# Attention's TensorE products issued in source order, in a block of a mixture of experts, attention and a second mixture

## The chip, the cores and the metric

The kernel runs on one core of a Trainium2 chip, in float32 throughout. A core has TensorE (matrix products, PE, with its weight loads PEld), VectorE (DVE), ScalarE (ACT), GpSimd (POOL) and SyncE (SP), which run side by side, each in the order of its own queue, and 16 DMA engines. Products land in PSUM, which has eight banks of 2 KB in each partition; all else lies in SBUF. The metric is the device time of one execution in microseconds (us), the median of some runs.

## The reference

Three residual steps on x of 2 x 1024 tokens with 512 features: half a mixture of experts, attention, half a mixture again. The change is in attention alone. Cut to what matters:

```python
x = x + 0.5 * ffn(layernorm(x))      # 2 experts, one per token, hidden 2048
x = x + attention(layernorm(x))
x = x + 0.5 * ffn(layernorm(x))

# attention: 16 heads, key width 64, value width 128, 64 slots a head
q, k, v = x @ Wq, x @ Wk, x @ Wv;  s = clip(x @ Ws, -32, 32);  g = x @ Wg
z = cumlogsumexp(s over time);  p = exp(s - z);  decay = exp(z[t-1] - z[t])
hk = hk * decay + k_t p_t^T          # per head, 64 x 64
ok_t = q_t hk / sqrt(64);  pv = softmax(ok over the slots)
hv = hv * decay + p_t v_t^T          # per head, 64 x 128
o_t = pv_t hv
o = rmsnorm(o) * g_norm_weight * g * sigmoid(g)
return o @ Wo
```

## The kernel before

Python code writes the whole program out without loops on the chip. A planner (the Tile framework) then sets the order of each engine's queue: it goes through the instructions with a time model of its own, gives an engine the earliest written one that is ready in the model, and adds all waits between engines. So the order on an engine may differ from that of the source. `tc.issue_after(ins)` binds instructions: what is written inside its block is put behind `ins` on the engine of `ins`, and adds no wait by itself. PSUM is guarded by bank. Pools give a tile name a number of buffers (`bufs`); a new tile waits until the last user of its buffer is done.

The first mixture runs to about 510 us, attention to 1965 us, the last mixture (its first steps inside attention's last units) to the end.

Attention works on 64 *units*: 2 sequences x 4 groups of 4 heads x 8 chunks of 128 tokens (c = 0 to 7). The state of a group is carried from chunk to chunk in `sk_st` and `sv_st`. Iteration i of the main loop (L1273) works on three units at once: *cur* is unit i, *mid* i-1, *old* i-2. An 8-chunk group repeats the same pattern.

Projections are made for two neighbouring units together, by a scheme with 7 products of half matrices in place of 8, as generators of which `next` takes a step:

- `values_gates` (L968): v and the gate sg of a pair, with banks U (tag ok), C and V (tag pj). The sums X of the tokens that it needs are made by DVE in `token_sums`. A product is 2 matmuls of 128x128 by 512 columns.
- `keys_slots` (L1015): k and E, the exponentials of the slots, of a pair. U and V are the two halves of one bank, `bank[:, 0]` and `bank[:, 1]`. ACT copies partial sums out (kp, kv, ku, L1024), DVE adds (L1033, L1042). A product is 2 matmuls by 256 columns.
- `queries` (L1057): once for 4 chunks, pq, 8 matmuls by 512 columns.

In an odd iteration the values of a later pair are made, in an even one the keys of *cur* and its neighbour, and the rest of the values.

The other products of a unit are small, each with a step of another engine behind it:

- `transpose_keys_slots` (tk), copied by ACT to kET; `running_sum` makes CT and its reciprocal rC on DVE.
- `scores` (Ap): products of 64 rows, two halves of the array one after the other in two banks (tag at, 2 buffers); DVE masks each to A (L1092).
- `slot_scores` (ok): for each of two pairs of heads the state product (sk, L1117, full array), then two products with A onto 64 columns each (L1122), all in one bank of tag at. DVE multiplies by rC to sT.
- `slot_softmax` (ts): transposes, maximum and subtraction on DVE, Exp on ACT to e.
- `transpose_u` (tu), DVE to uT; `update_key_state` (skp), DVE into sk_st.
- `slot_weights` (Bp): as Ap, masks to B. `outputs` (ov): state product (L1180), then products with B (L1186); ACT squares, DVE and ACT make the norm ms, POOL scales the gate sg (L1201), DVE multiplies to og (L1203).
- `update_value_state` (svp): products onto 64 columns each, DVE adds into sv_st. ts, skp and svp share one bank (tag st), to, tu and tk another (tag tr).
- `transpose_out` (to), ACT to oT; `project_out` (po): 4 matmuls by 512 columns, DVE adds to the rows x. In the last group it also calls `then.feed()`, which ranks finished tokens for the last mixture.

A matmul over all rows and columns of the array shows as 128*128 in the profile; Ap and Bp are 64*128, svp and the products of L1122 128*64. One fp32 product shows as two records, a transpose as one.

Source order of an iteration before: ok(mid); a projection step; ts(mid), to(old); steps; tu(mid), po(old); skp(mid), Bp(mid); steps; ov(mid), svp(mid); tk, running sum, queries, Ap of cur. The planner was free to mix them.

Of the kernel before, what the change touches and what calls it, by code (L numbers as in the profile page):

```python
# [49 lines left out]
def tile_macaron(  # L50
# [783 lines left out]
    class Attention:  # L834
        def __init__(self, ph):
            self.ph, self.rows, self.xT = ph, [None] * NBLK, [None] * NBLK
            self.vg, self.ks, self.q, self.o = {}, {}, {}, {}

        def norm(self, b):
# [99 lines left out]
    def attention(att, then, then_steps, weight_steps):  # L939
# [3 lines left out]


        def product(bank, left, right, start):
            for d in range(2):
                nc.tensor.matmul(  # L947
                    bank, lhsT=left[:, d], rhs=right[:, d],
                    start=start and d == 0, stop=d == 1, skip_group_check=True,
                )  # L950
# [17 lines left out]
        def values_gates(u):  # L968
# [21 lines left out]
            p1 = keep(U, "th", "p1")  # L990
            token_sums(u)
            C = ps2.tile([P, 512], F32, tag="pj", name=f"C{u.nm}")
            product(C, a12, B21, True)
# [21 lines left out]
        def keys_slots(u):  # L1015
            pair = u, units[u.n + 1]
            B11, B21, B22, T1, T2, T3, T4 = att.ks[u.b, u.g]
            a11, a12, a21, a22 = halves(u)
            bank = ps2.tile([P, 2, 256], F32, tag="pj", name=f"kU{u.nm}")
            U, V = bank[:, 0], bank[:, 1]  # L1020

            def keep(bank, tag):
                t = work.tile([P, 256], F32, tag=tag, name=f"{tag}{u.nm}", bufs=1)
                nc.scalar.copy(t, bank)  # L1024
                return t

            def key(v):
                v.k = work.tile([P, HG * DK], F32, tag="k", name=f"k{v.nm}")
                return v.k

            def slot(v, bank, other):
                v.E = work.tile([P, HG * M], F32, tag="E", name=f"E{v.nm}", bufs=3)
                nc.vector.tensor_tensor(v.E, bank, other, ALU.add)  # L1033
                nc.vector.tensor_scalar(v.E, v.E, -32.0, 32.0, ALU.max, ALU.min)
                nc.scalar.activation(v.E, v.E, AF.Exp)


            product(U, a11, B11, True)
            p1 = keep(U, "kp")
            C = ps2.tile([P, 256], F32, tag="pj", name=f"kC{u.nm}")  # L1040
            product(C, a12, B21, True)
            nc.vector.tensor_tensor(key(u), C, p1, ALU.add)  # L1042
            product(V, u.S[:, 0], T1, False)
            p5 = keep(V, "kv")
            product(U, u.S[:, 1], T2, False)
            u2 = keep(U, "ku")
            product(V, u.S[:, 3], B22, False)
            slot(u, V, u2)
            yield
            product(U, u.S[:, 2], T3, False)  # L1050
            slot(pair[1], U, p5)
            yield
            product(U, a22, T4, False)
            nc.scalar.copy(key(pair[1]), U)
            yield

        def queries(u, prev):  # L1057
# [4 lines left out]
            for pr in range(NPR):  # L1062
                pj = ps2.tile([P, 512], F32, tag="pj", name=f"pq{u.nm}_{pr}")
                for dc in range(DC):
                    c0 = dc * HG * DK + pr * P
                    nc.tensor.matmul(  # L1066
                        pj, lhsT=att.q[u.b, u.g][:, c0 : c0 + P], rhs=xT[u.blk][:, dc, :],
# [4 lines left out]
        def transpose_keys_slots(u):  # L1072
            tp = ps1.tile([P, 2 * NPR, P], F32, tag="tr", name=f"tk{u.nm}")
            for pr in range(NPR):
                nc.tensor.transpose(tp[:, pr, :], u.k[:, ts(pr, P)], ident)
                nc.tensor.transpose(tp[:, NPR + pr, :], u.E[:, ts(pr, P)], ident)
            u.kET = work.tile([P, 2 * NPR, P], F32, tag="kET", name=f"kET{u.nm}", bufs=3)
            nc.scalar.copy(u.kET, tp)

        def masked_products(u, name, lT, rT):  # L1080
# [3 lines left out]
            for j in range(2):  # L1084
                r = slice(j * 64, (j + 1) * 64)
                pp = ps2.tile([P, NPR, P], F32, tag="at", name=f"{name}p{u.nm}_{j}")
                for pr in range(NPR):
                    nc.tensor.matmul(
                        pp[:, pr, :], lhsT=lT[r, pr, :], rhs=rT[r, pr, :],
                        start=True, stop=True,  # L1090
                    )
# [20 lines left out]
        def slot_scores(u):  # L1112

            op = ps2.tile([P, NPR, P], F32, tag="at", name=f"ok{u.nm}")
            for pr in range(NPR):
                if u.c:
                    nc.tensor.matmul(  # L1117
                        op[:, pr, :], lhsT=sk_st[:, pr, :],
                        rhs=u.qT[:, pr, ts(u.c % 4, P)], start=True, stop=False,
                    )  # L1120
                for j in range(2):
                    nc.tensor.matmul(  # L1122
                        op[j * M : (j + 1) * M, pr, :],
                        lhsT=u.E[:, ts(2 * pr + j, M)], rhs=u.A[:, j * NPR + pr, :],
                        start=(u.c == 0), stop=True,
                    )
# [3 lines left out]
        def slot_softmax(u):  # L1130
            tp = ps1.tile([P, HG, M], F32, tag="st", name=f"ts{u.nm}")
            for pr in range(NPR):
                nc.tensor.transpose(
                    tp[:, 2 * pr : 2 * pr + 2, :].rearrange("p h m -> p (h m)"), u.sT[:, pr, :], ident
# [10 lines left out]
        def update_key_state(u):  # L1145
# [3 lines left out]
            for pr in range(NPR):  # L1149
                nc.tensor.matmul(  # L1150
                    sp[:, pr, :], lhsT=u.k[:, ts(pr, P)], rhs=u.E[:, ts(pr, P)],
# [10 lines left out]
        def transpose_u(u):  # L1162
            tp = ps1.tile([P, NPR, P], F32, tag="tr", name=f"tu{u.nm}")
            for pr in range(NPR):
                nc.tensor.transpose(
                    tp[:, pr, :], u.u[:, 2 * pr : 2 * pr + 2, :].rearrange("p h m -> p (h m)"), ident
# [9 lines left out]
        def outputs(u):  # L1176
            op = ps1.tile([P, HG, DV], F32, tag="ov", name=f"ov{u.nm}")
            for pr in range(NPR):
                if u.c:
                    nc.tensor.matmul(  # L1180
                        op[:, 2 * pr : 2 * pr + 2, :].rearrange("p h v -> p (h v)"),
                        lhsT=u.uT[:, pr, :], rhs=sv_st[:, pr, :],
                        start=True, stop=False,
                    )
                for h in (2 * pr, 2 * pr + 1):
                    nc.tensor.matmul(  # L1186
                        op[:, h, :], lhsT=u.Bm[:, h % 2 * NPR + pr, :], rhs=u.v[:, ts(h, DV)],
                        start=(u.c == 0), stop=(u.c == 0 or h % 2 == 1),
                    )

# [12 lines left out]
            nc.vector.tensor_tensor(u.og, op, sg, ALU.mult)  # L1203

        def update_value_state(u):
            if u.c == NC - 1:
                return
            sp = ps1.tile([P, NPR, DV], F32, tag="st", name=f"svp{u.nm}")
            for h in range(HG):
                j = h % 2  # L1210
                nc.tensor.matmul(  # L1211
                    sp[j * M : (j + 1) * M, h // 2, :],
                    lhsT=u.E[:, ts(h, M)], rhs=u.v[:, ts(h, DV)], start=True, stop=True,
                )
            for j in range(2):
                r, v = slice(j * M, (j + 1) * M), ts(j, DV)
                st = sv_st[r, :, v]
                if u.c == 0:
                    nc.vector.tensor_copy(st, sp[r, :, :])
                else:  # L1220
                    nc.vector.tensor_tensor(st, sp[r, :, :], st, ALU.add)  # L1221

        def transpose_out(u):
            tp = ps1.tile([P, HG, P], F32, tag="tr", name=f"to{u.nm}")
            for h in range(HG):
                nc.tensor.transpose(tp[:, h, :], u.og[:, h, :], ident)  # L1226
            u.oT = work.tile([P, HG, P], F32, tag="oT", name=f"oT{u.nm}")
            nc.scalar.activation(u.oT, tp, AF.Copy, scale=gnh)  # L1228

        def project_out(u):  # L1230
# [3 lines left out]
            for h in range(HG):  # L1234
                nc.tensor.matmul(  # L1235
                    pj, lhsT=u.oT[:, h, :], rhs=att.o[u.b, u.g][:, ts(h, D)],
# [33 lines left out]

        for _ in range(3):
            project_ahead(-1)
        for i in range(n + 2):  # L1273
# [3 lines left out]

            def step():
                if i >= n - 1:
                    next(then_steps)  # L1280

            if mid:
                slot_scores(mid)
            if cur:
                if i % 2:
                    project_ahead(i)
                else:
                    keys = keys_slots(cur)
                    next(keys)
            step()  # L1290
            if mid:
                slot_softmax(mid)
            if old:
                transpose_out(old)
            if cur:
                project_ahead(i)
                if i % 2 == 0:
                    next(keys)
            step()
            if mid:  # L1300
                transpose_u(mid)
            if old:
                project_out(old)
            step()
            if mid:
                update_key_state(mid)
                slot_weights(mid)
            if cur:
                project_ahead(i)
                if i % 2 == 0:  # L1310
                    ahead = None
                    next(keys)
            step()
            if mid:
# [3 lines left out]
                if mid.b == 0 and mid.c < 6 and mid.g < NG - 1:  # L1318
                    with tc.issue_after(mid.gated.ins):
                        next(weight_steps)  # L1320
                        next(weight_steps)
            step()
            if cur:
                transpose_keys_slots(cur)
                running_sum(cur, mid)
                queries(cur, mid)
                scores(cur)
                if cur.g == NG - 1 and cur.b == 0:
# [96 lines left out]
```

## Time and profile before

| what | us |
|---|---|
| median of 3 runs | 2398.35 (2397.66 to 2399.46) |
| the profiled execution, as timed | 2399.73 |
| its span, from first to last instruction | 2398.0 |
| TensorE busy in the span | 2333.1 |
| one pattern of 8 units, from the same product at 761.56 to that at 940.90 | 179.3 |
| TensorE busy from 1200 to 1300 | 99.85 |
| DVE busy from 1200 to 1300 | 61.23 |
| ACT busy from 1200 to 1300 | 39.59 |
| POOL busy from 1200 to 1300 | 8.26 |

The profile is of one execution. In its timelines a row is: start, length, engine, line, operation, what is written <- what is read, shapes, and how many records were merged into the row; brackets hold the engine's idle time before it and what ended that. The length of a TensorE row goes to the modelled end of its last product, which overlaps the next row: distances between starts tell how long TensorE was held. In the waits a row is: who waited <- for whom: us in total, times, longest.

### The profile page before, as it was taken

What the parts mean: (1) busy time and instruction counts of PE and PEld (TensorE: products, weight loads), DVE (VectorE), ACT (ScalarE), POOL (GpSimd) and SP (SyncE); (2) the same over time, 40 slices, a digit from 0 to 9 for tenths busy, and PEclk for the clock granted to TensorE, in tenths of its full rate; (3) what the DMA queues carried; (4) which work ended last, traced back from release to release, by engine and by line L of the source; (5) the groups of instructions that cost most, each with busy time, mean ns of one, the idle gap of its engine ahead of it and who ended that gap; (6) DMA issues with size and microseconds to landing.
All of it is one profiled execution on the core that took longest, in us unless ns stands there. A gap on an engine that the chain in (4) does not pass through costs nothing.

```text
span 2398.0 us, 28205 instructions
## 1 busy us (share of the span) xinstructions
PE 2333.1 (97%) x10552; PEld 1566.3 (65%) x10552; DVE 1366.1 (57%) x3116; ACT 784.1 (33%) x1470; POOL 466.6 (19%) x401
## 2 busy tenths in 40 slices
PE   7998999999999999999999999999999999999998
PEld 5686787865555556556556556556556578888865
DVE  6543556656546556557666545555557567766411
ACT  2221222323333333344443333333333432222222
POOL 3513616101101101100101000000000244634000
PEclk9999999999999999999999999999999999999999
DMA  7516335221311311310401200200100203313442
GB/s 286 211 64 247 142 106 213 75 103 45 123 57 44 127 54 45 110 58 23 163 27 49 80 27 14 80 27 14 62 1 36 106 18 154 106 62 132 158 171 97
DMA packets 56937, 222.70 MB, mean 93 GB/s; under 512 B 5983, under 2 KB 13151, under 8 KB 38880
## 3 DMA queue, kind: packets, MB, share of 16 engines
q1 hardware_dynamic: 51232, 203.52, 23.9%
q0 software_dynamic: 5280, 16.85, 1.8%
q8 instruction: 83, 1.36, 0.2%
q10 hardware_dynamic: 288, 0.52, 0.1%
q14 instruction: 54, 0.44, 0.1%
HBM read 189.86 MB, written 31.54 MB: 92 GB/s over the span
## 4 chain that ended last, share of the span: by engine, by line
PE 81%; DVE 10%; issue 5%; DMA 2%; POOL 1%; ACT 1%; SPq 0%; POOLq 0%; DVEq 0%; ACTq 0%
PE U L947 9%; PE po L1235 9%; PE kU L947 6%; PE oa L673 6%; PE hU L606 6%; PE V L947 5%; PE pq L1066 5%; PE o L673 4%; PE hp L509 4%; PE hV L606 3%; PE op L728 3%; PE C L947 2%; PE ok L1122 2%; PE ov L1186 2%; PE ov L1180 2%
## 5 line engine op out<-in xcount | busy, mean ns | idle before, releaser
L1201 POOL TENSOR_TENSOR sg<-sg,ms 128x512 f32<-128x512 f32 x64 | 66.5, 1039 | 1202.8 <-DVE ms L1199 1177.4
L1235 PE MATMUL po<-wo,oT 128*128 128x512 f32 x512 | 232.5, 593 | 0.6 <-ACT oT L1228 0.6
L509 PE MATMUL hp<-xsT,wfc 128*128 128x256 f32 (+1 forms) x768 | 150.6, 352 | 10.6 <-DMA wfc<-in_w_fc_dram 7.2
L509 PEld LDWEIGHTS hp<-xsT,wfc 128*128 128x128 f32 x768 | 129.0, 194 | 33.6 <-issue 15.4
L1235 PEld LDWEIGHTS po<-wo,oT 128*128 128x128 f32 x512 | 92.2, 191 | 88.2 <-issue 86.4
L728 PE MATMUL op<-wp,a 128*128 128x512 f32 x320 | 143.2, 593 | 0.0
L947 PE MATMUL U<-vgT,X 128*128 128x512 f32 x256 | 125.5, 593 | 0.0
L496 DVE SCALAR_TENSOR_TENSOR t<-hp,r 128x256 f32<-128x256 f32 (+1 forms) x96 | 36.3, 379 | 155.4 <-ACT r L495 155.1
L1240 DVE TENSOR_TENSOR x<-po,x 128x512 f32<-128x512 f32 x64 | 44.3, 691 | 136.6 <-PE po L1235 136.6
L1066 PE MATMUL pq<-xnT,wq 128*128 128x512 f32 x256 | 112.9, 593 | 0.0
L1110 DVE RECIPROCAL rC<-CT 128x256 f32<-128x256 f32 x64 | 111.6, 1744 | 0.3
L947 PE MATMUL kU<-ksT,X 128*128 128x256 f32 x384 | 105.8, 393 | 0.6 <-ACT kp L1024 0.6
L986 ACT ACTIVATE th<-sg 128x512 f32<-128x512 f32 x64 | 40.2, 629 | 183.9 <-DVE sg L984 183.6
L606 PE MATMUL hU<-xsT,wfc 128*128 128x256 f32 x384 | 100.0, 383 | 0.3 <-ACT e L613 0.3
L728 PEld LDWEIGHTS op<-wp,a 128*128 128x128 f32 x320 | 59.8, 191 | 60.8 <-issue 57.3
L947 PEld LDWEIGHTS kU<-ksT,X 128*128 128x128 f32 x384 | 68.5, 190 | 31.7 <-DVE E L1033 10.6
L495 ACT ACTIVATE r<-hp 128x256 f32<-128x256 f32 (+1 forms) x96 | 33.3, 347 | 156.5 <-PE hp L509 156.1
L1197 ACT ACT_TABLE_LOAD x55 | 70.6, 1283 | 41.8 <-DVE ms L1196 41.8
L1221 DVE TENSOR_TENSOR sv<-svp,sv 64x256 f32<-64x256 f32 x96 | 40.4, 421 | 76.9 <-PE svp L1211 74.7
L1186 PEld LDWEIGHTS ov<-v,B 128*128 128x128 f32 x512 | 76.5, 191 | 10.2 <-issue 3.3
L1228 ACT ACTIVATE oT<-to,gnh 128x512 f32<-128x512 f32 x64 | 43.6, 681 | 120.6 <-PE to L1226 120.3
L1066 PEld LDWEIGHTS pq<-xnT,wq 128*128 128x128 f32 x256 | 47.4, 191 | 52.7 <-issue 52.5
(296 smaller groups left out, 5168.2 us busy)
## 6 DMA issues: line engine op xcount, KB each, us to landing
wfc<-in_w_fc_dram SPq DMA_DIRECT2D x48, 1024.0 KB, 4.9
wp<-in_w_proj_dram SPq DMA_DIRECT2D x48, 1024.0 KB, 6.6
vgT<-vgs SPq DMA_DIRECT2D x16, 1024.0 KB, 5.2
wv<-in_w_v_dram SPq DMA_DIRECT2D x8, 1024.0 KB, 6.2
ksT<-kss SPq DMA_DIRECT2D x8, 1024.0 KB, 4.7
wo<-in_w_o_dram SPq DMA_DIRECT2D x8, 1024.0 KB, 6.1
xs<-xs SPq DMA_DIRECT2D x6, 1032.0 KB, 6.2
wks<-in_w_ks_dram SPq DMA_DIRECT2D x24, 256.0 KB, 4.1
```

Of the source, the lines that this page charges most:

```text
L509: m.mark = nc.tensor.matmul(hp, lhsT=wfc[:, dc * HQ + hc * P : dc * HQ + (hc + 1) * P], rhs=xT[:, dc, :], start=(dc == 0), stop=(dc == DC ...
L606: m.mark = nc.tensor.matmul(bank, lhsT=left[:, d, :], rhs=right[:, d, :], start=start and d == 0, stop=d == 1, skip_group_check=True,)
L673: nc.tensor.matmul(bank[:, t, :], lhsT=left(q)[:, ts(t, P)], rhs=right(q), start=first and q == 0 and (t == 0 or last), stop=last and q == ...
L728: nc.tensor.matmul(ops[j], lhsT=a[hc][:, ts(j, P)], rhs=wp[:, ts(hc, D)], start=(ck == 0 and hc == 0), stop=(ck == NHQ - 1 and hc == HQ // ...
L947: nc.tensor.matmul(bank, lhsT=left[:, d], rhs=right[:, d], start=start and d == 0, stop=d == 1, skip_group_check=True,)
L1066: nc.tensor.matmul(pj, lhsT=att.q[u.b, u.g][:, c0 : c0 + P], rhs=xT[u.blk][:, dc, :], start=(dc == 0), stop=(dc == DC - 1),)
L1110: nc.vector.reciprocal(u.rC, u.CT)
L1122: nc.tensor.matmul(op[j * M : (j + 1) * M, pr, :], lhsT=u.E[:, ts(2 * pr + j, M)], rhs=u.A[:, j * NPR + pr, :], start=(u.c == 0), stop=True,)
L1186: nc.tensor.matmul(op[:, h, :], lhsT=u.Bm[:, h % 2 * NPR + pr, :], rhs=u.v[:, ts(h, DV)], start=(u.c == 0), stop=(u.c == 0 or h % 2 == 1),)
L1197: nc.scalar.activation(ms, ms, AF.Sqrt, bias=eps, scale=1.0 / DV)
L1201: u.gated = then.gated = nc.gpsimd.tensor_tensor(sg, sg, ms.to_broadcast([P, HG, DV]), ALU.mult)
L1235: nc.tensor.matmul(pj, lhsT=u.oT[:, h, :], rhs=att.o[u.b, u.g][:, ts(h, D)], start=(h == 0), stop=(h == HG - 1),)
```

## The change

All of attention's products and transposes go through a helper that puts each one behind the one traced just before it. The generators of the projections get three more places to stop. `slot_scores` and `outputs` do all state products before the local ones (with flags that fit), `value_state_products` is taken out of `update_value_state` and put behind `slot_weights`, `update_key_state` goes ahead of `slot_weights` by a projection step, `transpose_out` goes ahead of `slot_softmax`, and `project_out` goes behind `queries`. The steps of the last mixture that run beside the last units stay five to an iteration.

```diff
+        def on_pe(op, *args, **kw):
+            with tc.issue_after(att.pe.ins) if att.pe else nullcontext():
+                att.pe = op(*args, **kw)
...
         def product(bank, left, right, start):
             for d in range(2):
-                nc.tensor.matmul(
+                on_pe(
+                    nc.tensor.matmul,
                     bank, lhsT=left[:, d], rhs=right[:, d],
...
         def values_gates(u):
             token_sums(u)
+            yield
             C = ps2.tile([P, 512], F32, tag="pj", name=f"C{u.nm}")
...
         def keys_slots(u):
             nc.vector.tensor_tensor(key(u), C, p1, ALU.add)
+            yield
             product(V, u.S[:, 0], T1, False)
             p5 = keep(V, "kv")
             product(U, u.S[:, 1], T2, False)
             u2 = keep(U, "ku")
+            yield
             product(V, u.S[:, 3], B22, False)
...
         def slot_scores(u):
+            for pr in range(NPR if u.c else 0):
+                on_pe(
+                    nc.tensor.matmul, op[:, pr, :], lhsT=sk_st[:, pr, :],
+                    rhs=u.qT[:, pr, ts(u.c % 4, P)], start=(pr == 0), stop=False,
+                    skip_group_check=True,
+                )
             for pr in range(NPR):
-                if u.c:
-                    nc.tensor.matmul(
-                        op[:, pr, :], lhsT=sk_st[:, pr, :],
-                        rhs=u.qT[:, pr, ts(u.c % 4, P)], start=True, stop=False,
-                    )
                 for j in range(2):
-                    nc.tensor.matmul(
-                        op[j * M : (j + 1) * M, pr, :],
+                    on_pe(
+                        nc.tensor.matmul, op[j * M : (j + 1) * M, pr, :],
                         lhsT=u.E[:, ts(2 * pr + j, M)], rhs=u.A[:, j * NPR + pr, :],
...
+        def value_state_products(u):
+            if u.c == NC - 1:
+                return
+            u.svp = ps1.tile([P, NPR, DV], F32, tag="st", name=f"svp{u.nm}")
+            for h in range(HG):
+                j = h % 2
+                on_pe(
+                    nc.tensor.matmul, u.svp[j * M : (j + 1) * M, h // 2, :],
+                    lhsT=u.E[:, ts(h, M)], rhs=u.v[:, ts(h, DV)], start=True, stop=True,
+                )
...
-        for _ in range(3):
+        for _ in range(4):
             project_ahead(-1)
```

The main loop after, in full up to the loads, which stay as they were:

```python
            def project(even, odd):
                if i >= n - 1:
                    next(then_steps)
                for step in (odd if i % 2 else even) if cur else "":
                    if step == "v":
                        project_ahead(i)
                    else:
                        next(keys)

            if cur and i % 2 == 0:
                keys = keys_slots(cur)
            project("k", "v")
            if mid:
                slot_scores(mid)
            project("k", "v")
            if old:
                transpose_out(old)
            if mid:
                slot_softmax(mid)
            project("kvk", "v")
            if mid:
                transpose_u(mid)
                update_key_state(mid)
            project("k", "v")
            if mid:
                slot_weights(mid)
                value_state_products(mid)
            project("v", "")
            if cur and i % 2 == 0:
                ahead = None
            if mid:
                outputs(mid)
                update_value_state(mid)
                ...
            if cur:
                transpose_keys_slots(cur)
                running_sum(cur, mid)
                queries(cur, mid)
            if old:
                project_out(old)
            if cur:
                scores(cur)
```

## The prediction

> **What bounds the kernel now.** I read the busy table and the slices first, then the chain, the waits of TensorE, and last the timeline of the attention stage (about 510 to 1965 us).
>
> ```profile
> span 2398.0 us, 28205 instructions
> PE 2333.1 (97%) x10552; PEld 1566.3 (65%) x10552; DVE 1366.1 (57%) x3116; ACT 784.1 (33%) x1470; POOL 466.6 (19%) x401
> PEclk9999999999999999999999999999999999999999
> PE 81%; DVE 10%; issue 5%; DMA 2%; POOL 1%; ACT 1%; SPq 0%; POOLq 0%; DVEq 0%; ACTq 0%
> DVE og L1203 <- POOL sg L1201: 54.2, 53, 1.2
> PE ok L1117 <- DVE A L1092: 6.5, 18, 1.0
> PE kU L947 <- ACT kp L1024: 0.6, 1, 0.6
> ```
>
> TensorE sets the time: 97% busy at the full granted clock, and in attention it waits for hardly anything (the last two lines, of the waits: us in total, times, longest; the line on DVE is used further down). So an order of its work can win only in how long the same products take, and lose only by new waits. The first is in the timeline of TensorE (start, length, line, records merged; one fp32 matmul is two records):
>
> ```profile
> 943.08 1.02 PE L947 MATMUL U<-vgT,X 128*128 128x512 f32 x2
> 944.03 0.43 PE L1122 MATMUL ok<-A,E 128*64 128x128 f32 x2
> 944.40 0.49 PE L1117 MATMUL ok<-qT,sk 128*128 128x128 f32 x2
> 944.82 0.44 PE L1122 MATMUL ok<-A,E 128*64 128x128 f32 x4
> 945.18 1.13 PE L947 MATMUL kU<-ksT,X 128*128 128x256 f32 x4
> ...
> 953.48 0.61 PE L1150 MATMUL skp<-E,k 128*128 128x128 f32 x4
> 954.02 0.72 PE L1088 MATMUL Bp<-uT,kET 64*128 64x128 f32 x8
> 954.67 1.98 PE L947 MATMUL U<-vgT,xnT 128*128 128x512 f32 x4
> ```
>
> Read the starts. Undisturbed, a full-array (128*128) record takes 0.43 us at 512 columns, 0.215 at 256, 0.108 at 128 (four skp records: 0.54 with what follows). But 943.08 to 944.03 is 0.95 for two records of 0.43: 0.10 more, because what follows uses half the array (128*64). The half-array records then end 0.15 late, and the first full-array record afterwards is 0.11 long (945.18: four records in 0.97 instead of 0.86). Each *excursion* to a half-array form costs this toll beside its work. I took it over all 363 excursions of attention from the matmul starts, from the full record before to the second one after, less the undisturbed times (half-array records counted at 53 ns, since two halves can run together): ok in 2 records 0.459 us (90 times; only one half is in use), ok in 4 records 0.367 (67), ok in all 8 0.364 (8), Bp in 8 0.430 (63), Ap in 8 0.440 (44), Ap in 4 0.405 (32), svp in 8 0.318 (51), svp run into Ap 0.630 (4; 0.589 median), odd ones 2.0 us. Sum 148.9 us.
>
> **What the change takes away.** Every attention matmul is put behind the one traced before it, and slot_scores now does its four state records first. So ok becomes one excursion of 8 for each of 64 units, Ap one of 8, and Bp with svp right behind it one of 16 (56 units; 8 last chunks have no svp). Priced by the rows: ok 64 x 0.363 = 23.2; Ap 64 x 0.427 (median) = 27.3; Bp+svp 56 x 0.589 = 33.0; Bp alone 8 x 0.429 = 3.4. Sum 86.9, so **62 us** less. The Bp+svp price is bounded by the four run-on pairs (0.589) and by two full tolls (0.429 + 0.363 = 0.79).
> The Trainium skill, "TensorEngine Tiling (Array Packing)", section Key Properties, says that changing the tiling mode, not just the tile, drains TensorE; Bp (64*128) to svp (128*64) changes it. By that rule the pair would pay 0.79, the sum of gains would be 11 us smaller and the time 2390.
> The old waits of ok and kU go too: 6.5 + 0.6, and the 0.11 us restart that I count 45 times behind a state product of ok that had to wait, and 37 times behind kU and U: 4.9 + 4.0. About **16 us**. Gains together 78 (62 to 78; 51 with two tolls).
>
> **What it adds.** Matmuls and their columns stay the same, value_state_products only moves; no DMA is added, and loads, stores and weight sums keep their places in the SP and POOL queues. The flags and the wrapper cost no instruction. project_out moves behind tk and queries; in the last group the feed (DVE, a ranking matmul, POOL scatters) goes with it. The last scatter now starts at 1970.97 and pass 1's tokens are worked on at 2009, so some us there are covered; without cover they would be paid once. What counts is that TensorE can no longer step past an instruction that waits. Place by place:
>
> 1. *Keys, second step* (32 pairs). U and V share a bank, and the planner lets no engine write one half while another reads the other:
>
> ```profile
> 1033.02 0.35 ACT L1024 COPY kp<-kU 128x256 f32<-128x256 f32 x1
> 1033.43 1.13 PE L947 MATMUL kU<-ksT,X 128*128 128x256 f32 x4 [0.63 <-ACT kp L1024]
> ...
> 1034.39 1.02 PE L947 MATMUL U<-vgT,X 128*128 128x512 f32 x2
> 1034.59 0.37 ACT L1024 COPY kv<-kU 128x256 f32<-128x256 f32 x1 [1.22 <-PE kU L947]
> ...
> 1035.25 1.03 PE L947 MATMUL kU<-ksT,X 128*128 128x256 f32 x4
> ```
>
> At 1033.43 product V waits for the copy kp of U, though they share no data. Between V and the next U there is now always a product of values (1034.39), which hides the copy kv. After the change V and U stand back to back in one step with nothing between: 0.20 us to the copy's start, 0.37, 0.06 to TensorE, 0.11 restart: 0.74. 32 x 0.74 = **23.7** (nothing in the row hides it; zero only if the planner tracked halves).
> 2. *Keys, third step*: the copy ku needs 0.74 in the same way, transposes of 6 x 0.109 = 0.65 lie before: 0.1 x 32 = **3**.
> 3. *Keys, last step*: U waits for DVE's add of E (0.42). The add starts 0.34 us after its product on average (0.20 to 0.76); 0.34 + 0.42 + 0.06 + 0.11 less the cover of 0.65 (tu, skp) is 0.28: 32 x 0.3 = **10** (4 to 20).
> 4. *ok after Ap* (48 units; the other 16 have a query projection as cover). Behind tk: kET ready 0.79 later, then on DVE CT 2 x 0.46 and rC 1.74 (with small ones done 4.2 us after tk), the add x 0.69, the masks A 0.42 each. TensorE in that time: po 3.44, Ap 0.85, one step 1.72: ok starts at 6.0 and needs both masks at 6.4. They are there at 5.8 if they go first. But og may stand in the queue ahead of them, and DVE waits there for POOL:
>
> ```profile
> 1011.47 1.74 DVE L1110 RECIPROCAL rC<-CT 128x256 f32<-128x256 f32 x1
> ...
> 1013.48 0.15 DVE L1199 TENSOR_TENSOR ms<-ms,rs 128x4 f32<-128x4 f32 x1
> 1013.71 1.04 POOL L1201 TENSOR_TENSOR sg<-sg,ms 128x512 f32<-128x512 f32 x1 [18.23 <-DVE ms L1199]
> 1014.78 0.69 DVE L1203 TENSOR_TENSOR og<-ov,sg 128x512 f32<-128x512 f32 x1 [1.15 <-POOL sg L1201]
> ```
>
> sg from 4.35 to 5.4, og to 6.1, masks to 7.0: ok 0.75 late. I take 0.3, nearer to the first, since the add x fills most of POOL's time: 48 x 0.3 = **14** (0 to 67, see the rivals).
> 5. *Softmax*: ts to e takes 3.05 us in the median (two DVE steps of 0.42, a table load 1.28, Exp 0.41 and the copy oT before them); the cover is three steps, 4 x 0.86 = 3.44. Some 10% of units run over: 64 x 0.05 = **3** (0 to 12).
> 6. *Outputs of a first chunk* (8) have only svp ahead of the masks B, which are done 0.99 after Bp: 8 x 0.3 = **2**. The last two units, where only steps of the second mixture are left to fill: **2** (0 to 6).
>
> Others are covered: uT (0.65) by skp and a step (1.3 or more), sT (0.54) by a step and the transposes (2.1), og (7.65 after ov) by 9.4 of TensorE's work, k and E by whole steps.
>
> Sum: 2398.0 - 78 + (24 + 3 + 10 + 14 + 3 + 2 + 2 = 58) = 2378 for the span. The profiled run is 2399.73 as timed, the median 2398.35; on the median the forecast is **2379**, 0.8% faster. Its own range, from 51 to 78 of gain and the likely part of the costs, is 2365 to 2393.
>
> **Rivals.**
> *The planner puts the DVE order well*: masks first, E at once. Then places 1, 2 and 6 stay (24 + 3 + 4) and 7 us for the rest: 2398 - 78 + 38 = 2358. For it: DVE is 57% busy. Against: 53 waits of og for POOL, 1.0 us each, show that DVE does stand behind a slow POOL.
> *og ahead of everything on DVE* (the slower case). If og is queued even before the add x, both masks come at 7.7 and ok's state product, which needs Ap's bank, is about 1.4 late with restart, in 48 units: 67 instead of 14. Time 2398 - 78 + 44 + 67 = 2431; with the add first in a third of the units, 2418. From 0.7 us per unit on (34 of net gain without it, over 48) the kernel is slower. For it: the planner's idea of POOL's time is too short, as those waits show. Against: x is ready 0.7 us before sg even starts.
> *Gains and costs cancel* (two tolls for Bp+svp and 9 us more of waits): 2398, within 0.2%.
> *The change doesn't hold the chains together*: only attention's own products are ordered, and norms or the second mixture may come between. That touches some 16 of 64 units: a fourth of 62 is lost, and with fillers that tear all chains half, 31 + 16 - 58: 2409.
>
> **How the numbers follow.** Forecast 0.38, good DVE order 0.18, cancel 0.11, og first 0.28, not held together 0.05. A change under 0.2% (5 us) can't be told from none here. Faster 0.38 + 0.18 = 0.56; same 0.11; slower 0.28 + 0.05 = 0.33. Range 2350 to 2420: it leaves out a tenth below and a tenth above.
>
> **What would show it.** Right: excursions fall from 363 to about 192 with no ok in 2 records; a wait of 0.6 us of kU for kv appears 32 times; PE busy falls by more than the span. Wrong: kU waits for nothing (halves tracked), ok waits for A by more than 0.7 us in most units, or the attention stage keeps its 22.4 us per unit although the excursions are gone, for a reason that I haven't listed, such as a transfer that comes late.

## The result and the profile after

The kernel after takes 2398.31 us in the median of 12 runs (2394.33 to 2400.97), beside 2398.79 of the kernel before on the same chip: a ratio of 0.9995, with a 95% interval of 0.9986 to 1.0004. Nothing is gained that can be measured; the forecast was 2379. The head of the profile after, with the busy times and the chain that ended last:

```profile
span 2395.6 us, 28304 instructions
PE 2288.2 (96%) x10552; PEld 1553.9 (65%) x10552; DVE 1385.9 (58%) x3116; ACT 774.0 (32%) x1462; POOL 468.9 (20%) x401
PEclk9999999999999999999999999999999999999999
PE 63%; DVE 17%; issue 12%; POOL 4%; DMA 2%; ACT 2%; SPq 0%; POOLq 0%; DVEq 0%; ACTq 0%
```

TensorE is busy for 45 us less, in a span that is only 2.4 us shorter. The time is no longer in its rows but between them: DVE, POOL and ACT have 23% of the chain where they had 12%. The six largest waits of TensorE for attention (who waited <- for whom: us in total, times, longest):

```profile
PE kU L949 <- ACT kv L1034: 13.3, 29, 0.5
PE ok L949 <- DVE A L1106: 10.1, 26, 0.8
PE Bp L949 <- DVE uT L1187: 8.4, 25, 3.5
PE kU L949 <- DVE E L1043: 4.2, 14, 0.5
PE to L949 <- ACT xnT L207: 4.1, 6, 0.7
PE tu L949 <- ACT e L1156: 1.0, 2, 0.5
```

Of the six, ok for A and tu for e stood in the list of before too (6.5 in 18 waits, 1.2 in one); the other four are new. Three of the places stand within 12 us of TensorE's timeline (start, length, line, records merged; in brackets the idle time and what ended it):

```profile
896.73 0.71 PE L949 MATMUL ok<-qT,sk 128*128 128x128 f32 x4 [0.17 <-DVE A L1106]
897.38 0.66 PE L949 MATMUL ok<-A,E 128*64 128x128 f32 x8
897.96 1.13 PE L949 MATMUL kU<-ksT,X 128*128 128x256 f32 x4
899.56 1.13 PE L949 MATMUL kU<-ksT,X 128*128 128x256 f32 x4 [0.46 <-ACT kv L1034]
...
905.44 1.13 PE L949 MATMUL kU<-ksT,xnT 128*128 128x256 f32 x4
906.76 0.72 PE L949 MATMUL Bp<-uT,kET 64*128 64x128 f32 x8 [0.20 <-DVE uT L1187]
907.41 0.66 PE L949 MATMUL svp<-v,E 128*64 128x128 f32 x8
```

The excursions are as the change writes them: ok in one of 8 records, Bp with svp behind it. But at 899.56 product U waits for the copy of V, at 896.73 ok for its mask, at 906.76 Bp for uT. What of TensorE's time is not the undisturbed time of its matmuls, from 460 us to the end, by the prediction's reckoning from starts:

| us | excursions | their toll | all other lost time | both |
|---|---|---|---|---|
| before | 363 | 148.9 | 71.5 | 220.4 |
| after | 193 | 102.6 | 113.3 | 215.9 |

The toll falls by 46.3 and the rest rises by 41.8. By stages (start of the first tk transpose of a unit), the length of each in us; *let go* and *source alone* are experiments of the next section:

| stage | before | after | let go | source alone |
|---|---|---|---|---|
| start to unit 8 | 691.2 | 689.8 | 685.1 | 681.2 |
| units 8 to 24 | 359.2 | 351.7 | 350.7 | 343.0 |
| 24 to 32 (the norm of the second sequence runs beside) | 181.2 | 188.3 | 179.1 | 179.1 |
| 32 to 56 | 536.6 | 526.5 | 524.3 | 512.8 |
| 56 to the end (the last mixture begins) | 629.9 | 639.2 | 633.7 | 633.9 |

So the change does gain, in the mean 3.4 to 3.8 us in each 8 steady units, and gives it back in two places: 7.1 us where the norm's products stand between attention's, 9.3 after unit 56.

### The profile page after: what moved, and what is told of

It reads as the page before. It is cut to its first block, busy times and chain, and to the rows that moved or that the text cites. A ratio compares the mean times of both kernels' runs of the same rounds, so it can differ in the third digit from the quotient of the medians.

```text
span 2395.6 us, 28304 instructions
## 1 busy us (share of the span) xinstructions
PE 2288.2 (96%) x10552; PEld 1553.9 (65%) x10552; DVE 1385.9 (58%) x3116; ACT 774.0 (32%) x1462; POOL 468.9 (20%) x401
## 4 chain that ended last, share of the span: by engine, by line
PE 63%; DVE 17%; issue 12%; POOL 4%; DMA 2%; ACT 2%; SPq 0%; POOLq 0%; DVEq 0%; ACTq 0%
PE U L949 7%; PE oa L673 6%; PE hU L606 6%; PE o L673 4%; PE kU L949 4%; PE ov L949 4%; PE V L949 4%; PE pq L949 3%; PE hp L509 3%; PE hV L606 3%; DVE rC L1124 3%; PE op L728 3%; PE po L949 3%; PE ok L949 2%; PE C L949 2%
## 5 line engine op out<-in xcount | busy, mean ns | idle before, releaser
L949 PE MATMUL U<-vgT,X 128*128 128x512 f32 x256 | 120.3, 592 | 0.0
L606 PEld LDWEIGHTS hU<-xsT,wfc 128*128 128x128 f32 x384 | 72.3, 191 | 14.6 <-issue 3.8
L949 PEld LDWEIGHTS U<-vgT,X 128*128 128x128 f32 x256 | 48.6, 190 | 47.6 <-issue 45.9
L1210 DVE TENSOR_REDUCE ms<-sq 128x4 f32<-128x512 f32 x64 | 43.8, 685 | 58.6 <-ACT sq L1208 58.6
```

The costliest lines, as they stand in the source:

```text
L606: m.mark = nc.tensor.matmul(bank, lhsT=left[:, d, :], rhs=right[:, d, :], start=start and d == 0, stop=d == 1, skip_group_check=True,)
L949: att.pe = op(*args, **kw)
L1210: nc.vector.tensor_reduce(ms, sq, AX.X, ALU.add)
```

## The experiments

The theories were: the strict order puts TensorE behind late results where the planner used to step past (then letting go of the order gains); the places of the products in the new source are bad in themselves (then letting go gains nothing); and the order is what keeps the small chains whole (then letting go brings back the torn chains). "Toll" is the excursions' toll as above. Every ratio is to the kernel before on the same chip, with its 95% interval; the chips differ (the kernel before takes 2396.77 to 2398.91 on them), so medians of different runs compare to some 2 us.

**1. `order_let_go`: the order between chains let go of in two stages only** (`fresh` is called first in each small function and in `product`).

```diff
+        def fresh():
+            if att.free:
+                att.pe = None
...
+            att.free = 24 <= i <= 32 or i >= 56
```

> The changed kernel, but attention's products are bound to one another only inside each chain, not from chain to chain, in iterations 24 to 32 (where the second sequence is normalized) and from 56 to the end (where the last mixture begins). Theory A: the order earns 3.7 us in each group of 8 units and loses it at these two places, because TensorE can't step past a product that waits for ScalarE's or VectorE's work of the norm or of the mixture. Then the first place gains 8 to 11 us and the second 8 to 13: 2375 to 2383 us. Theory B: the losses there are work that only moved, and the gain is eaten by the new waits in every unit (kU for kv, ok for A, Bp for uT): 2395 to 2401 us.

2377.11 us, 0.9917 (0.9903 to 0.9930), 195 excursions. The norm stage is 9.2 us shorter than after and shorter than before, the end stage 5.5, less than expected. Of the rest, 4.7 lie ahead of attention, where the two kernels don't differ (scatter between two executions), and 3.2 in the two stages between. So in these two stages it is the order that costs, and the chains stay whole without it.

**2. `keys_split`: V and U of the keys in different steps.**

```diff
             p5 = keep(V, "kv")
+            yield
             product(U, u.S[:, 1], T2, False)
...
-            project("v", "")
+            project("kv", "")
```

> The changed kernel with one more place to stop in keys_slots, between the copy kv and the next product of U; out, softmax's transposes now lie between them, and the last step of the keys goes behind svp. If the wait for kv (29 times, 0.63 us with the restart) is paid in full, 18 us go and some 3 to 6 us come back in the step that now has to wait for VectorE's add of E: 2383 to 2388 us. If the wait only moves to the next place on ScalarE's or VectorE's queue: 2395 to 2400 us.

2389.63 us, 0.9975 (0.9966 to 0.9984): the waits for kv fall from 29 to one of 0.5, yet the gain is less than expected: 7 us under before, and under after 9 by the medians, 5 by the ratios. Waits of TensorE:

```profile
PE Bp L949 <- DVE uT L1188: 10.0, 32, 3.5
PE ok L949 <- DVE A L1107: 10.0, 26, 0.8
PE ts L949 <- DVE sT L1145: 3.7, 5, 0.8
```

The step between tu and Bp is now another product of the keys, and the add of the E before it stands in DVE's queue ahead of uT: Bp waits 32 times instead of 25. sT is now waited for, and the norm's transposes (ln) wait 4.2 us for DVE where they waited 0.8. In a fixed order a mended wait uncovers the next.

**3. `both`: the two edits together, the order let go of in the same two stages.**

> Both edits. Theory A: their gains add, 2360 to 2372 us. Theory B: as the split of the keys alone, 2380 to 2388 us.

2366.46 us, 0.9870 (0.9855 to 0.9885), 197 excursions: 30 us under before on the same chip, where the two edits alone give 20 and 7. The gains add up, within the intervals.

**4. `source_only`: the new source, bound only inside a chain, everywhere** (`att.free = True` throughout).

> The changed kernel's source, chains bound only inside themselves everywhere: the planner may mix them as before. If the binding from chain to chain is what keeps the chains whole: over 280 excursions to half of the array in place of 193, their toll back over 110 us, waits of TensorE in attention down to some 10 us, and 2385 to 2400 us. If the new source is enough by itself: under 230 excursions and 2365 to 2380 us.

2351.81 us, 0.9812 (0.9799 to 0.9826), below both forecasts, with 197 excursions and a toll of 95.2. That the binding from chain to chain keeps the chains whole is refuted: without it the planner leaves them whole, once the source writes each in one piece. The toll is 53.7 less than before, the other lost time 77.2, nearly that of before. Its timeline of TensorE at the keys' steps:

```profile
926.56 1.13 PE L949 MATMUL kU<-ksT,X 128*128 128x256 f32 x4
927.52 0.38 PE L949 MATMUL ts<-ident,sT 128*128 128x128 f32 x2
927.74 1.02 PE L949 MATMUL U<-vgT,X 128*128 128x512 f32 x2
928.60 1.03 PE L949 MATMUL kU<-wks,X 128*128 128x256 f32 x4
929.47 1.02 PE L949 MATMUL U<-vgT,X 128*128 128x512 f32 x2
930.32 1.03 PE L949 MATMUL kU<-ksT,X 128*128 128x256 f32 x4
```

Between two products of the keys the planner puts half a product of values, which hides the copy. In the list of waits kv, xnT and all of uT but the one in the last units are gone; this one stays:

```profile
PE ok L949 <- DVE A L1114: 10.6, 26, 0.9
```

**5. `order_only`: the old source with every product of attention bound to the one before.** All its nc.tensor calls go through `on_pe` as after; nothing moves.

> The kernel before, with its own source order, and every attention product bound behind the one traced before it; nothing else. Theory C: the change has two parts of opposite sign, the new source (-46 us, as the run with the new source and no binding between chains showed) and the binding from chain to chain (+46). The old source has far less behind its chains (five products of the keys in one step, Ap right behind the transposes of keys and slots): the binding then costs over 100 us, 2480 to 2600 us, with waits of ok for A, kU for kv and ku, Ap for kET. Rival: the binding costs about the same on any source, since the planner's order is near the source's: 2400 to 2450 us.

2712.04 us, 1.1301 (1.1282 to 1.1320): 313 us slower, above the forecast too, with 300 excursions and 347.7 us lost in them by the same reckoning, the waits within them included. Waits of TensorE, then its timeline in one unit:

```profile
PE ok L948 <- DVE A L1097: 107.3, 109, 1.8
PE Ap L948 <- ACT kET L1083: 34.2, 46, 1.7
PE kU L948 <- ACT ku L1029: 14.3, 31, 0.5
PE kU L948 <- ACT kv L1029: 14.3, 31, 0.5
```

```profile
1216.51 0.72 PE L948 MATMUL Ap<-qT,kET 64*128 64x128 f32 x8 [0.68 <-ACT kET L1083]
...
1218.69 0.49 PE L948 MATMUL ok<-qT,sk 128*128 128x128 f32 x2 [0.88 <-DVE A L1097]
1219.11 0.43 PE L948 MATMUL ok<-A,E 128*64 128x128 f32 x2
1221.30 0.69 PE L948 MATMUL ok<-A,E 128*64 128x128 f32 x2 [1.75 <-DVE A L1097]
...
1223.27 3.78 PE L948 MATMUL U<-wv,xnT 128*128 128x512 f32 x4
```

In the old source ok stands right behind Ap, and a strict order waits there for each mask. The last row is a further cost: such a row of U is 1.98 us long at the full clock and 3.78 here (see the last section).

**6. `ok_whole`: before, with only the state-first slot_scores, bound inside.**

```diff
+            for pr in range(NPR if u.c else 0):
+                on_pe(
+                    op[:, pr, :], lhsT=sk_st[:, pr, :],
+                    rhs=u.qT[:, pr, ts(u.c % 4, P)], start=(pr == 0), stop=False,
+                )
             for pr in range(NPR):
-                if u.c:
...
```

> The kernel before with one edit: slot_scores makes its state products first and is bound inside itself. Theory D: the torn ok chains (165 excursions, 69 us of toll) were most of what the new source mends. If the planner leaves the chain in one piece: some 64 excursions of 8, toll down by up to 45 us, 2353 to 2370 us. Rival: without the finer steps and the later po the planner has nothing to put between Ap and ok, and the chain, which now starts only when both masks are there, waits: 2385 to 2400 us with more wait of ok for A.

2382.00 us, 0.9929 (0.9913 to 0.9946): less than expected. 307 excursions, toll 128.3: 44 of the chains are torn in 2 and 6 records, since the second mask is late (behind DVE's rC) and the planner fills with something else. Binding inside fixes the order of a chain's products, and doesn't keep others out.

**7. `state_between`: source_only with the old form of slot_scores** (state, local, local for each pair).

> The new source bound only inside chains, but slot_scores in its old form, with a state product ahead of each pair of heads. Each unit but the first of a group then has two excursions of 4 records, 0.367 us each, in place of one of 0.377: 56 x 0.36 = 20 us more than with the new form. Theory D (the ok chain is the main part): 2370 to 2378 us. If the planner tears it further: 2385 us and more. If it is the rest of the source that earns: 2352 to 2362 us.

2371.91 us, 0.9890 (0.9874 to 0.9907), 253 excursions, toll 115.5: 20 us above `source_only`, as is the toll. State first is worth that much of the 45 that `source_only` gains.

**8. `unbound`: source_only, bound only inside ok and outputs.**

> The new source with nothing bound but the products inside ok and inside ov. If binding inside the other chains did nothing but what the planner does anyway: 2350 to 2355 us and about 197 excursions. If the planner tears Ap, Bp and svp when it may: over 220 excursions and 2358 to 2370 us.

2354.17 us, 0.9809 (0.9793 to 0.9826), toll 94.6: the same. Binding inside the other chains does nothing.

**9. `po_back`: source_only with the output projection in its old place.**

```diff
             if mid:
                 transpose_u(mid)
+            if old:
+                project_out(old)
+            if mid:
                 update_key_state(mid)
...
-            if old:
-                project_out(old)
```

> The new source bound only inside chains, with project_out where it was before, right behind transpose_u. Ap then follows the transposes of keys and slots and queries at once, and VectorE's reciprocal rC (1.75 us) has no 3.4 us of TensorE's work in front of the masks. If the later place of po is what gives ok its cover: waits of ok for A over 20 us and torn ok chains again, 2365 to 2385 us. If the planner, free again, finds other cover: 2350 to 2357 us.

2368.26 us, 0.9875 (0.9860 to 0.9890). The 3.4 us of po are taken from between tk and Ap. ok waits only 1.0 us in all, but 258 excursions cost 124.6: with less ahead of ok, its chains are torn (ok in 2 and 6, Ap in 4). A planner that may fill pays for a missing cover in torn chains, not in waits.

**10. `svp_back`: source_only with svp behind the outputs, apart from Bp.**

```diff
                 slot_weights(mid)
-                value_state_products(mid)
...
                 outputs(mid)
+                value_state_products(mid)
```

> The new source bound only inside chains, with the products for the value state behind those of the outputs, as before. 55 excursions Bp+svp of 0.591 us become Bp of 0.43 and svp of 0.32 to 0.36: 9 to 11 us more by the tolls, 2360 to 2364 us. If a change of the array's form in the middle of an excursion were paid in full, there would be no difference: 2350 to 2354 us.

2353.18 us, 0.9811 (0.9796 to 0.9826): the same as `source_only`, against expectation. The toll does rise by 16.1, to 111.3: two full tolls, 0.427 for Bp and 0.319 for svp, against 0.589 for the run-on pair, and nine of the svp chains are torn. It is paid back elsewhere: all other lost time falls by 15, since ok's waits for A fall from 10.6 us to 2.7 (from 17.4 to 4.5 with the restarts). DVE's queue shows why:

```profile
1255.19 0.69 DVE L1277 TENSOR_TENSOR x<-po,x 128x512 f32<-128x512 f32 x1
...
1255.87 0.75 DVE L1114 TENSOR_TENSOR A<-Ap,causal 128x256 f32<-128x256 f32 x2
1257.17 0.69 DVE L1232 TENSOR_TENSOR og<-ov,sg 128x512 f32<-128x512 f32 x1 [0.55 <-POOL sg L1230]
```

Of the 48 units without a query projection, 32 now have both masks ahead of og, which waits for POOL; in `source_only` and in the kernel after 6 have, and in 41 og stands ahead of both. (In before the planner had put both masks ahead in 45, in `po_back` in 46.) So the equal times are a coincidence of two effects, and the next two runs move og alone.

**11. `og_late`: source_only with the multiplication `og` written behind `scores(cur)`.**

```diff
+            u.op, u.gate = op, sg
+
+        def gate_outputs(u):
             u.og = work.tile([P, HG, DV], F32, tag="og", name=f"og{u.nm}")
-            nc.vector.tensor_tensor(u.og, op, sg, ALU.mult)
+            nc.vector.tensor_tensor(u.og, u.op, u.gate, ALU.mult)
...
                 scores(cur)
+            if mid:
+                gate_outputs(mid)
```

> The new source bound only inside chains, with VectorE's product og traced behind scores instead of in outputs, so that the two masks A stand ahead of it in VectorE's queue. In the run before this one the queue is x, og (which waits 0.43 us for GpSimd), A, A, and ok waits for A 26 times, 10.6 us, with a restart of 0.1 us each. If og's place is the cause: those waits fall under 3 us and the time to 2337 to 2344 us. If the masks are late for rC and x alone, or the wait goes to the transposes of og: 2349 to 2356 us.

2333.08 us, 0.9728 (0.9715 to 0.9741): 64 us better than before, below the forecast, the best of all. DVE in the kernel after, then in this one (same columns, DVE's rows):

```profile
935.53 0.69 DVE L1261 TENSOR_TENSOR x<-po,x 128x512 f32<-128x512 f32 x1
936.65 0.69 DVE L1219 TENSOR_TENSOR og<-ov,sg 128x512 f32<-128x512 f32 x1 [0.43 <-POOL sg L1217]
937.26 0.75 DVE L1106 TENSOR_TENSOR A<-Ap,causal 128x256 f32<-128x256 f32 x2
```

```profile
898.91 0.69 DVE L1280 TENSOR_TENSOR x<-po,x 128x512 f32<-128x512 f32 x1
899.52 0.75 DVE L1114 TENSOR_TENSOR A<-Ap,causal 128x256 f32<-128x256 f32 x2
900.19 0.68 DVE L1235 TENSOR_TENSOR og<-ov,sg 128x512 f32<-128x512 f32 x1
```

After, and in `source_only` with the same lengths (x at 921.53), DVE stands for POOL's sg with both masks queued behind; here the masks go first, in all 48 units without a query projection, and by the time of og the gate is there: DVE's waits of og for sg fall from 61 to 19. ok's waits for A are 0.3 us in all, and the other lost time is 58.9 instead of 77.2.

**12. `bound_og_late`: the same edit in the kernel after, order kept.**

> The changed kernel as it is, all products bound one behind the other, with og traced behind scores. The prediction's step 4 held that ok is late in the bound order because og, which waits for GpSimd, stands ahead of the masks A, at 14 us in all; the changed kernel shows 10.1 us of waits of ok for A in 26 places and restarts of some 0.1 us. If that is the cause, those waits fall under 3 us and the time by 10 to 20 us against the changed kernel, to 2378 to 2388 us. If the masks moved ahead make og, and with it out's transposes, late in a bound order: 2395 to 2402 us.

2379.42 us, 0.9922 (0.9908 to 0.9935), 19 us under after's median (17 by the ratios), and ok waits for A 0.3 us in all. The order of DVE's queue is worth the same with TensorE's order kept or let go of (`og_late` is 19 under `source_only`).

## Why the prediction was wrong

**The step that failed is the sentence "Others are covered: uT (0.65) by skp and a step (1.3 or more)"**: a term put at nothing cost some 8 us, half of the 16 us that are missing from the 62 of toll. The toll fell by 46.3. Against the forecast of 86.9 the excursions cost 102.6: ok 24.7 for 23.2, Ap 29.8 with two torn ones for 27.3, and the Bp groups 48.1 for 36.4. The pair's price was right: in `source_only` Bp with svp measures 0.591 in the mean for a forecast 0.589. So the 0.79 that the prediction drew from the Trainium skill's rule ("TensorEngine Tiling (Array Packing)", Key Properties), by which a change of the tiling mode drains TensorE, was too high; the two tolls apart measure 0.746 in `svp_back`. What the after kernel pays on top is Bp's wait for uT inside the excursion, 25 times (8.4 us by the list of waits, 11.7 from start to start). One of them, 3.5 us in the last unit, belongs to the 2 us that the prediction gave the last two units; DVE is busy for 9.96 of the 10 us from 1931, ahead of it. The other 8.2 us are the uncovered uT, late in every second unit. (In the 8 last chunks there is no skp to cover it, and Bp's excursion costs 0.69 for 0.43.) What is left of the 16 lies in ok and Ap. DVE's rows show why a cover of 1.3 us didn't do:

```profile
904.97 0.41 DVE L1043 TENSOR_TENSOR E<-kU,kv 128x256 f32<-128x256 f32 x1
905.30 0.17 DVE L1159 RECIPROCAL rs<-rs 128x4 f32<-128x4 f32 x1
905.48 0.69 DVE L996 SCALAR_TENSOR_TENSOR sg<-th,sg 128x512 f32<-128x512 f32 x1
906.09 0.29 DVE L1044 TENSOR_SCALAR E<-E 128x256 f32<-128x256 f32 x1
906.29 0.42 DVE L1187 TENSOR_TENSOR uT<-tu,rC 128x256 f32<-128x256 f32 x1
```

The transposes of u are followed by the next product at 904.91, but uT starts 1.4 us later, behind four instructions, three of them of the projections (E twice, sg). I counted uT's own work and an idle DVE. At place 4 I had looked at DVE's queue; here I had not. No run moved uT alone in that queue; with the planner free (`source_only`) all these waits but the last are gone.

**The sum of the added waits came out right, and so did its largest parts; the small ones did not.** Net of the old waits 42 was forecast (58 - 16), 41.8 measured. Below, a wait is counted as the prediction did, from the starts: the delay of the product and its restart. The list of waits shows less, since it counts from the modelled end of the product before.

- Place 1, kv: right, 29 waits of 0.73, 21.2 us for 23.7. `keys_split` (all but one) and `source_only` (all) remove it as the mechanism says.
- Place 2: 3 forecast, one wait of 0.7 found. Place 3: 10 forecast, 8.0 in 14 waits.
- Place 4, ok behind masks behind og: 14 forecast, 17 measured (10.1 in the list), and 17 to 19 us back when og is moved. The cause is the one named, shown by two kernels. That the number is near is in part luck: 0.3 a unit was taken as nearer to masks first, but og went first in 41 of 48 units, and that cost mostly 0.44 (the row at 896.73) and not the 0.75 reckoned for it.
- Place 5: 3 forecast, two waits of tu, 1.5. Place 6: no wait of a first chunk's outputs is in the list; the last two units are spoken of above.
- Not in the sum: the norm of the second sequence, where to waits for the copy xnT 6 times (4.1 us in the list; the two use one bank tag), and the end. The waits for xnT come to 5.4 of the 7.1 us given back there, and letting go of the order brings them back. In the end stage the 3.5 us wait for uT (at 1943 us) is one part, with the granted clock at 0.78 in the 5 us behind it; `source_only` has such a wait and such a dip too and loses 4.1 there against before, so part of that loss is the new source's and not the order's. It was not taken apart further.

**The rivals.** "Gains and costs cancel" gave 2398 and is the time that came, but by luck in half of it: its two tolls for the pair did not happen, its further waits did. Of "The planner puts the DVE order well", the masks first are what `bound_og_late` makes by hand; it stays 21 us above that rival's 2358, since waits at the other places remain. "og first" did not come: in the rows shown x goes ahead of og, and the place costs 17 to 19 us, not 67. "The change doesn't hold the chains together" is refuted: 193 excursions, none of ok in 2.

**The deeper fault was to price the change as one thing.** It has two parts that the prediction never separated: the source's new grouping, and the binding of each product to the one before. The grouping alone gives -45 us (`source_only`), the binding alone +313 (`order_only`), the binding on top of the new grouping +46 by the medians (44 by the ratios). I took the binding for what keeps chains whole. The runs show that binding from chain to chain adds nothing to that (within ok and the outputs, the products stayed bound in every run of the new source), and that it takes from TensorE the freedom to step past a late result, which the planner had been using all along.

## What to carry to other kernels

Write each small chain in one piece in the source and bind it, at most, inside: a total order over an in-order engine must be bought place by place with covers, and each one must include the queue of the engine that makes the late result, not only its own work. Price grouping and ordering apart, since one may earn what the other spends. On the engine in between, put what waits for a slow engine (og for POOL) behind what the bounding engine waits for (the masks): that alone was worth 17 to 20 us, with the strict order and without.

## What the runs showed of the hardware

**The clock fell with no long wait.** In `order_only` no wait of attention's products on TensorE is longer than 1.8 us, yet the granted clock is halved in 53 stretches, 294.7 us in all. Three of these have their like in before (two in the first mixture, one at the end of the span); from 500 to 1930 us before and after show none. Ahead of three more, TensorE waited 2.7 to 3.8 us for a ranking product (rp) of the last mixture. The other 47 follow no wait of 2 us. Three windows of it in a row (us, then busy time of PE, PEld, DVE, ACT and POOL with counts, granted clock, DMA share, GB/s):

```profile
1218.00:1221.40 3.40, 0.95 (x5) 0.59 (x6) 3.21 (x7) 0.44 (x1) 1.04 (x1) 0.98 0.22 82
1221.40:1224.80 3.40, 3.40 (x10) 1.82 (x11) 0.42 (x1) 0.00 (x0) 0.00 (x0) 0.50 0.00 0
1224.80:1228.20 3.40, 3.40 (x5) 1.35 (x4) 0.00 (x0) 0.58 (x1) 0.00 (x0) 0.52 0.00 0
```

TensorE was busy for 0.95 of 3.40 us, in pieces, and then had half its clock while it was fully busy. In the 3.4 us ahead of the 47 drops it was 25 to 55% busy. TensorE's rows fill 267 of the 294.7 us; if the work in them went at half its pace, 134 of the 313 us were lost so, an estimate (in before 13 us of rows lie in such stretches). The Trainium skill ("TensorE: Matmul & The Clock Gate", A second HAM failure mode: psum-queue depth-cycling) tells of a clock that swings because of many short idle times; these rows agree. The same page's rule of no idle gap above 3.4 us (section HAM oscillation — how this bites in real kernels) would have seen no danger at the 47. In the kernel after, with waits of at most 0.8 us in the steady units, the clock stays full there, and falls once in attention, behind the 3.5 us wait in the last units.

**DVE's sums beside POOL.** The sums X of 128x256 take 0.41 us, but up to 1.5 beside POOL's sums of weights (kernel after, timeline of both engines):

```profile
937.93 0.41 DVE L971 TENSOR_TENSOR X<-xnT 128x256 f32<-128x256 f32 x1
937.93 1.54 POOL L860 TENSOR_TENSOR G<-gw,G 128x512 f32<-128x512 f32 x1
938.26 1.50 DVE L973 TENSOR_TENSOR X<-xnT 128x256 f32<-128x256 f32 x1
...
940.01 0.41 DVE L972 TENSOR_TENSOR X<-X,xnT 128x256 f32<-128x256 f32 x1
```

Here the X that starts together with POOL's sum keeps its 0.41; the one that starts inside it ends 0.3 us after it. Before, all 12 of the long ones lie beside POOL's sums. No run separated the two, so that POOL is the cause is argued, not shown.
